# Two moves in a fused conditional-FFN kernel: the mixed 128x128 kernels get small tiles and ScalarE's DMA queue, and the inputs of the quarter products of a round's first pair are made on VectorE

## The chip, the cores and the metric

The kernel runs on one core of one Trainium2 chip. The metric is the device time of the whole program in microseconds. Before the change the median of three runs is 2623.2 us (2620.95 to 2623.56). A separate execution under the hardware profiler gives the trace.

## What is computed

The reference has two layers on x of 32 batches by 128 channels by 2048 positions, all in float32, each layer added to x. Cut to what matters:

```python
# layer 0
att   = softmax(mlp(cond))                              # 32 x 8
agg_w = einsum('bk,koi->boi', att, weight)              # a mixed 128x128 kernel for each batch
y     = einsum('boi,bih->boh', agg_w, x) + (att @ bias_k)[:, :, None]
x     = x + y @ W.T + bias + LoRA(y)                    # W is 2048 x 2048
# layer 1
z     = grouped_conv1d(x, 9 taps, 4 groups) + ctx + fside
x     = x + unpermute(ffn(permute(z)))                  # 16 heads: 128 -> 512, gelu, 512 -> 128
```

The kernel first folds the LoRA part into W, then multiplies x by W (positions by positions, 2048 by 2048), and applies the small mixed kernel of each batch afterwards, since the two products act on different axes.

## The kernel before, in words

**Rounds and steps.** The product x W is made by Strassen's scheme, two levels deep everywhere and three levels deep in part. The outer level gives seven rounds, worked in the order P1, P2, P6, P7, P5, P3, P4 (`ROUNDS`). Each round has eight steps g = 0 to 7, one for each group of four batches; `steps` lists all 56, and the main loop (L1043) goes through them. In a step of the inner level, `multiply` (L333) makes seven products of four matmuls each, 128x512, into PSUM banks, and after each product VectorE adds the bank to accumulators in SBUF (L342; in round P1 ScalarE copies the first ones, L344). After each product but the last, `between(j)` puts other work in VectorE's order.

**Pairs.** In rounds P2, P6, P7, P5 and P3 (`THIRD`) most steps come in pairs g = 0 and 1, 2 and 3, and so on (`in_pair`), which go through `multiply_third` (L426). There the inner products P2 and P4 of both steps are not made directly; they are replaced by a third Strassen level across the two steps. The even step makes its five other products (L439) and their evacuations (L435). The odd step makes its own five and between them the seven "quarter" products of the pair (L450, 128x256), which are evacuated by L458. Their order in an odd step is fixed: product P1; quarters P1 and P2; product P5; quarters P6 and P5; product P6; quarters P7 and P3; product P3; quarter P4; product P7. Quarters P1, P2 and P4 read x as it is. Quarters P6, P5, P7 and P3 read `sq`, four combinations of the two steps' x that `third_inputs` (L410, operations at L417 to L420) makes, and the weights' quarters P_q that `third_weights` (L380) makes at a round's start: eight operations of 128x256 on GpSimd (L393 to L396), and four on VectorE that `between` issues in step 0 (L1109). Quarter P6 goes into the same bank as quarter P1, so it needs that bank's evacuation.

P5 is the one round where each product is added to two accumulators (`ADDED`), so that each evacuation is two VectorE operations.

**Who makes what ahead.** At the start of a step i, GpSimd is given `x_combine` of step i+1 (L296: in P6, P7, P5 and P3 pieces at L283, then four sums at L311 to L314), then in step 0 `third_weights`, then in an even step of a pair `third_inputs` on GpSimd for all rounds but P6. In P6 `third_inputs` is on VectorE and is issued after the even step's `multiply_third` (L1137). SyncE's queue loads x (L268), partial sums (L273) and, in the middle of a round, weights of the next (L507); GpSimd combines those (L283) and at the round's end makes the weights' inner sums `inner_weights` (L245, L252 to L256).

**Slots.** All the large tiles are slots of one pool: 24 slots of 8 KB for each partition (`slot`, L82). A new tile takes a slot whose former tile has no user left in the program's order, and its first writer waits until that former tile's last users are done. The order of instructions on each engine is the program's own; nothing is rescheduled.

**The mixed kernels.** `mixed_kernel(b, ks)` (L536) makes agg_w of batch b on VectorE: one multiplication (L544) and seven multiply-adds (L546), all 128x128. `between(0)` to `between(3)` make two of the eight each. Sixteen kernels share one large slot `ags`, and when the sixteenth is finished GpSimd's queue stores them to HBM (L548) in one DMA of 1 MB. Rounds P2 to P3 make six kernels each in steps 1 to 6, b = 0 to 29; P4 makes b = 30 and 31 in its steps 0 and 1. In P4 and after it, `mix_loads` (L550) loads each kernel back as a small tile `agl` from the pool `agp` (tag "ag", two buffers).

**After the rounds** comes the convolution and the FFN (L818 and L829), interleaved; the change doesn't touch their code.

Of the kernel before, what the change touches and what calls it, by code (L numbers as in the profile page):

```python
# [8 lines left out]
FP = mybir.dt.float32  # L9
# [7 lines left out]
P = 128  # L17
B = 32
L = 2048
QW = 512  # L20
KEXP = 8
# [7 lines left out]
NCH = L // P  # L29
# [3 lines left out]
NG = B // GB  # L33
# [22 lines left out]
def adaln_ffn_kernel(  # L56
# [16 lines left out]
    nc = tc.nc  # L73
# [3 lines left out]
    agp = ctx.enter_context(tc.tile_pool(name="agp", bufs=2))  # L77
# [4 lines left out]
    def slot(name, shape=(P, L)):  # L82
        return big.tile(list(shape), FP, name=name, tag="s")
# [11 lines left out]
    def scratch(name, shape=(P, L)):  # L95
        return dram.tile(list(shape), FP, name=name, tag=name)
# [12 lines left out]
    ag_d = [scratch(f"ag_d{i}") for i in range(B // NCH)]  # L109
# [32 lines left out]
    def a_scale(h, k0, k1):  # L142
        for c in range(2):
            cols = a_sb[h][:, c, :, k0:k1]
            nc.vector.tensor_scalar(cols, cols, wsc[:, c : c + 1], None, ALU.mult)
# [139 lines left out]
    def x_loads(r, g):  # L285
        return {
            "P1": lambda: [x_load(g, 0, 0)],
            "P2": lambda: [x_load(g, 0, 1)],
            "P6": lambda: [x_load(g, 1, 0), x_load(g, 1, 1), x_load(g, 0, 0)],
            "P7": lambda: [x_load(g, 0, 0), x_load(g, 1, 0)],  # L290
            "P5": lambda: [x_load(g, 1, 0), x_load(g, 1, 1)],
            "P4": lambda: [x_load(g, 1, 1)],
            "P3": lambda: [x_load(g, 0, 1), part_load("s2", g)],
        }[r]()

    def x_combine(r, g, ts):  # L296

        a = ts[0]
        tt = nc.gpsimd.tensor_tensor
        if r == "P6":  # L300

            b, a, c = ts
            pieces(b, b, a, ALU.add)
            pieces(a, b, c, ALU.subtract)
            part_store("s2", g, a)
        if r in ("P7", "P5", "P3"):
            pieces(a, a, ts[1], ALU.add if r == "P5" else ALU.subtract)
        xa[steps.index((r, g))] = a
        s = slot(f"s_{r}{g}", (P, 4, QW))
        a11, a12, a21, a22 = a[:, 0, 0], a[:, 1, 0], a[:, 0, 1], a[:, 1, 1]  # L310
        tt(s[:, 0], a21, a22, ALU.add)  # L311
        tt(s[:, 1], s[:, 0], a11, ALU.subtract)
        tt(s[:, 2], a11, a21, ALU.subtract)
        tt(s[:, 3], a12, s[:, 1], ALU.subtract)  # L314
        return {
            "P1": a11, "P2": a12, "P3": s[:, 3], "P4": a22,
            "P5": s[:, 0], "P6": s[:, 1], "P7": s[:, 2],
        }
# [88 lines left out]
    def in_pair(r, g):  # L407
        return r in THIRD and (r, g // 2) not in SKIP
# [124 lines left out]
    ags = {}  # L533
    late, ins, pms, xgs, x1ts, va, vb, hts, open_ = {}, {}, {}, {}, {}, {}, {}, {}, {}

    def mixed_kernel(b, ks):  # L536

        if b % NCH == 0 and ks[0] == 0:
            ags[b // NCH] = slot(f"ags_{b}", (P, NCH, P))
        ag = ags[b // NCH][:, b % NCH]  # L540
        for k in ks:
            att = att_bc[:, b * KEXP + k : b * KEXP + k + 1]
            if k == 0:
                nc.vector.tensor_scalar(ag, mix[:, 0], att, None, ALU.mult)  # L544
            else:
                nc.vector.scalar_tensor_tensor(ag, mix[:, k], att, ag, ALU.mult, ALU.add)  # L546
        if b % NCH == NCH - 1 and ks[-1] == KEXP - 1:
            nc.gpsimd.dma_start(ag_d[b // NCH], ags.pop(b // NCH).rearrange("p b c -> p (b c)"))  # L548

    def mix_loads(b):  # L550
        g, tp, s = b // GB, b % GB // 2, b % 2
# [487 lines left out]
    def olds_load(i):  # L1039
        r, g = steps[i]  # L1040
        olds[i] = [old and part_load(old, g) for old, _ in ADDED[r]]

    for i, (r, g) in enumerate(steps):  # L1043
        ri = i // NG
        last_round = ri + 1 == len(ROUNDS)
        if i + 1 < len(steps):
            if i + 1 not in xs:
                xs[i + 1] = x_loads(*steps[i + 1])
            if not last_round:
                lhs[i + 1] = x_combine(*steps[i + 1], xs.pop(i + 1))  # L1050
                if r in THIRD and g == 0:
                    quarters, quarter_ops = third_weights(r, rhs)
                if in_pair(r, g) and g % 2 == 0 and r != "P6":
                    sq = third_inputs(i, nc.gpsimd)
        if i == 0:
            olds_load(0)
        if i + 1 < len(steps) and not last_round:
            olds_load(i + 1)
        ahead = i + 2 < len(steps) and ri > 0 and not last_round
        if ahead and steps[i + 2][0] != "P6":  # L1060
            xs[i + 2] = x_loads(*steps[i + 2])
        if g == NG - (1 if ri else 2) and ri < len(ROUNDS) - 1:
            nxt = inner_weights(ROUNDS[ri + 1], [nxt[kc] for kc in range(4)])

        if ri == 0:
            ks = blocks[4 + 2 * g : 6 + 2 * g]
            if ks:
                two = [wt.pop(k) for k in ks]
                w_make_two(ks, two, sa[ks[0][0]], tb[ks[0][1]])
                made.extend(ks)  # L1070
                if g == 1:
                    a_scale(1, 0, 4)
                    sa[1] = a_combine(1, nc.gpsimd.tensor_tensor)
                if g == 3:
                    part, tb[0] = b_combine(0, nc.gpsimd.tensor_tensor)
                    for _ in range(4):
                        part()
                for k, t in zip(ks, two):
                    unsummed.append((k[1], t))
                    if k[:2] == (1, 0):  # L1080
                        nxt[k[2]] = t
        elif ri + 1 < len(ROUNDS):
            for k, combine in waiting.items():
                nxt[k] = combine()
            waiting = {}
            if 2 <= g < 6:
                waiting[g - 2] = outer_weights(ROUNDS[ri + 1], g - 2)

        if last_round and g == 0:
            late_loads()  # L1090
        if last_round and g == 2:

            late["te"] = mix.rearrange("p (k r) c -> p k r c", k=2)
            nc.sync.dma_start(mix.rearrange("p k c -> p (k c)"), te_d)
        k0 = 3 * (g - NG)
        if last_round:
            stage(k0, stage_first)

        def between(j):

            g0 = g - (not last_round)
            b = (ri - 1) * (NG - 2) + g0
            if ri > 0 and 0 <= g0 < NG - 2 and b < B and j < KEXP // 2:
                mixed_kernel(b, (2 * j, 2 * j + 1))
            if ri == 0 and j == 2:
                for k in blocks[6 + 2 * g : 8 + 2 * g]:
                    wt[k] = w_load(*k)
            if r in THIRD and j < 4 and quarter_ops:
                nc.vector.tensor_tensor(*quarter_ops.pop(0), ALU.subtract)  # L1109
            if j == 3 and ahead and steps[i + 2][0] == "P6":  # L1110
                xs[i + 2] = x_loads(*steps[i + 2])
            if ri == 0 and j in (1, 3) and unsummed:
                row_sums(*unsummed.pop())
            if ri == 0 and j == 5 and unsummed_first:
                t = unsummed_first.pop(0)
                tt = nc.vector.tensor_tensor
                tt(wsum[:, 0, 0], wsum[:, 0, 0], t[:, 0, 0], ALU.add)
                tt(wsum[:, 0], wsum[:, 0], t[:, 1], ALU.add)
            if last_round:
                if j == 3 and i + 1 < len(steps):  # L1120
                    lhs[i + 1] = x_combine(*steps[i + 1], xs.pop(i + 1))
                    olds_load(i + 1)
                if j in (2, 4):
                    stage(k0 + j // 2, stage_first)
                if j % 2:
                    stage_third(k0 + j // 2)
                else:
                    stage(k0 + j // 2, stage_second)

        if in_pair(r, g):  # L1130
            multiply_third(
                r, g, lhs.pop(i), rhs, olds.pop(i), between, quarters, sq if g % 2 else None
            )
        else:
            multiply(r, g, lhs.pop(i), rhs, olds.pop(i), between)
        xa.pop(i - 1, None)
        if in_pair(r, g) and g % 2 == 0 and r == "P6":  # L1137
            sq = third_inputs(i, nc.vector)
        next(chain, None)
        if i > 5:  # L1140
            next(chain, None)
        if last_round and g >= 6:
            pair(g - 6)
        if last_round and g == 7:
            rings()
            gather_two(0)
        if g == NG - 1 and ri + 1 < len(ROUNDS):
            rhs = nxt
            nxt = {}
# [84 lines left out]
```

## Time and profile before

| | |
|---|---|
| median of the runs | 2623.2 us (2620.95 to 2623.56) |
| profiled execution, its own time | 2625.11 us |
| its span, first to last instruction | 2623.0 us |
| mean granted TensorE clock | 0.994 |
| TensorE matmul | 2590.8 us, 99% |
| VectorE | 1459.2 us, 56% |
| GpSimd | 1337.5 us, 51% |
| ScalarE | 532.9 us, 20% |
| DMA | 608.27 MB, mean 232 GB/s |

The profile has several views, and all of them are of one execution. The head of the page gives each engine's busy time and its share of the span. The waits list who waited for whom: the engine with line and tile, the releaser, the total in us, the number of times, the longest. The timeline gives the instructions of an engine in order of time, with like ones merged: start, duration, engine, line, operation, output and inputs, shape, count, and in brackets the idle time of the engine before it with what ended it. PE is TensorE, PEld its weight loads, DVE VectorE, ACT ScalarE, POOL GpSimd, SP SyncE. A float32 matmul shows as two records. The round starts, read from the first product of each round on TensorE's timeline, are P2 306, P6 494, P7 681, P5 884, P3 1077 and P4 1261 us.

### The profile page before, as it was taken

What the parts mean: (1) busy time and instruction counts of PE and PEld (TensorE: products, weight loads), DVE (VectorE), ACT (ScalarE), POOL (GpSimd) and SP (SyncE); (2) the same over time, 40 slices, a digit from 0 to 9 for tenths busy, and PEclk for the clock granted to TensorE, in tenths of its full rate; (3) what the DMA queues carried; (4) which work ended last, traced back from release to release, by engine and by line L of the source; (5) the groups of instructions that cost most, each with busy time, mean ns of one, the idle gap of its engine ahead of it and who ended that gap; (6) DMA issues with size and microseconds to landing.
All of it is one profiled execution on the core that took longest, in us unless ns stands there. A gap on an engine that the chain in (4) does not pass through costs nothing.

```text
span 2623.0 us, 21287 instructions
## 1 busy us (share of the span) xinstructions
PE 2590.8 (99%) x6876; PEld 1310.3 (50%) x6876; DVE 1459.2 (56%) x2310; ACT 532.9 (20%) x1099; POOL 1337.5 (51%) x1110
## 2 busy tenths in 40 slices
PE   9999999999998999999999999999999999999998
PEld 4444455455454555455444445555545554555543
DVE  5554155455353476454376666676666666666610
ACT  0000000000000000000011244444444444444432
POOL 7320657987975773886432334434443344444222
PEclk9999999999998999999999999999999999999999
DMA  7542458778465577566668798777777777787532
GB/s 314 213 163 109 175 210 331 270 297 335 183 246 234 193 287 297 233 246 235 214 219 260 222 311 291 233 231 221 234 234 249 251 222 225 231 252 232 165 120 88
DMA packets 183838, 608.27 MB, mean 232 GB/s; under 512 B 17200, under 2 KB 88368, under 8 KB 139440
## 3 DMA queue, kind: packets, MB, share of 16 engines
q1 hardware_dynamic: 149936, 473.74, 51.1%
q0 software_dynamic: 32992, 132.14, 14.9%
q10 hardware_dynamic: 800, 1.03, 0.1%
q8 instruction: 55, 0.90, 0.1%
q14 instruction: 55, 0.45, 0.0%
HBM read 372.45 MB, written 200.84 MB: 219 GB/s over the span
## 4 chain that ended last, share of the span: by engine, by line
PE 78%; POOL 13%; DMA 5%; issue 2%; DVE 1%; SPq 0%; POOLq 0%; ACT 0%; DVEq 0%; ACTq 0%
PE bank L818 17%; PE bank L829 16%; PE bank L349 15%; PE bank L439 13%; PE bank L674 6%; PE bank L450 5%; POOL xt L283 5%; PE bank L582 4%; PE bank L223 2%; DMA xt<-in_xT 2%; POOL wo_P L283 1%; POOL wo_P L256 1%; DMA bf_sb<-in_BfT 1%; POOL P_t L253 1%; POOL s_P L311 1%
## 5 line engine op out<-in xcount | busy, mean ns | idle before, releaser
L818 PE MATMUL bank<-t,ws 128*128 128x512 f32 x1024 | 460.4, 592 | 0.6 <-DMA ws<-in_ffw 0.6
L829 PE MATMUL bank<-gl,ws 128*128 128x512 f32 x1024 | 460.2, 592 | 0.0
L836 POOL DMA_INDIRECT out<-t,orow x128 | 151.6, 1185 | 537.5 <-DVE t L834 458.6
L821 ACT ACTIVATE gl<-bank 128x512 f32<-128x512 f32 x512 | 306.2, 598 | 446.1 <-PE bank L818 443.1
L829 PEld LDWEIGHTS bank<-gl,ws 128*128 128x128 f32 x1024 | 194.6, 190 | 233.0 <-issue 230.8
L818 PEld LDWEIGHTS bank<-t,ws 128*128 128x128 f32 x1024 | 194.5, 190 | 227.5 <-issue 222.5
L567 POOL TENSOR_TENSOR x<-x,fb 128x512 f32<-128x512 f32 x128 | 178.7, 1424 | 213.5 <-DMA x<-in_x 175.7
L573 ACT ACTIVATE bank<-w,aggb 128x512 f32<-128x512 f32 x128 | 80.8, 683 | 916.9 <-DMA w<-w_d 900.0
L834 DVE TENSOR_TENSOR t<-bank,t 128x512 f32<-128x512 f32 x128 | 88.5, 691 | 319.7 <-PE bank L829 319.7
L439 PE MATMUL bank<-P_t,s_P 128*128 128x512 f32 x544 | 241.8, 592 | 0.0
L435 DVE TENSOR_TENSOR u<-bank,u 128x512 f32<-128x512 f32 x168 | 110.7, 688 | 199.6 <-PE bank L439 186.6
L283 POOL TENSOR_TENSOR xt<-xt,xt 128x512 f32<-128x512 f32 x128 | 162.4, 1302 | 92.3 <-DMA xt<-in_xT 82.9
L311 POOL TENSOR_TENSOR s_P<-xt 128x512 f32<-128x512 f32 x56 | 72.3, 1291 | 260.6 <-DMA xt<-in_xT 169.6
L439 PE MATMUL bank<-wo_P,s_P 128*128 128x512 f32 x448 | 199.1, 592 | 0.0
L546 DVE SCALAR_TENSOR_TENSOR ags<-mix,att_bc,ags 128x128 f32<-128x128 f32 x224 | 177.1, 791 | 4.5
L439 PEld LDWEIGHTS bank<-P_t,s_P 128*128 128x128 f32 x544 | 103.4, 190 | 115.6 <-issue 111.7
L802 POOL DMA_INDIRECT t<-hx_d,row x128 | 131.4, 1027 | 50.1 <-issue 26.4
L349 PE MATMUL bank<-P_t,s_P 128*128 128x512 f32 x352 | 154.7, 592 | 0.0
L439 PEld LDWEIGHTS bank<-wo_P,s_P 128*128 128x128 f32 x448 | 85.1, 190 | 95.2 <-issue 93.5
L674 PE MATMUL bank<-va,tw_l 128*128 128x256 f32 x512 | 121.6, 380 | 0.2
L674 PEld LDWEIGHTS bank<-va,tw_l 128*128 128x128 f32 x512 | 96.8, 190 | 41.9 <-issue 31.7
L450 PE MATMUL bank<-P_q,sq 128*128 128x256 f32 x408 | 101.3, 401 | 16.4 <-DVE u L458 9.8
(189 smaller groups left out, 3563.4 us busy)
## 6 DMA issues: line engine op xcount, KB each, us to landing
xt<-in_xT SPq DMA_DIRECT2D x88, 1024.0 KB, 9.1
u<-u_d SPq DMA_DIRECT2D x40, 1024.0 KB, 8.5
wo_P<-wb_d SPq DMA_DIRECT2D x36, 1024.0 KB, 10.9
u<-c_d SPq DMA_DIRECT2D x64, 512.0 KB, 7.1
x<-in_x SPq DMA_DIRECT2D x32, 1024.0 KB, 8.5
xg<-x SPq DMA_DIRECT2D x256, 128.0 KB, 5.4
hx_d<-x1t SPq DMA_DIRECT2D x32, 1024.0 KB, 5.9
hx_d<-ht SPq DMA_DIRECT2D x32, 1024.0 KB, 7.1
```

The costliest lines, as they stand in the source:

```text
L283: nc.gpsimd.tensor_tensor(out[:, i, j], a[:, i, j], b[:, i, j], op)
L349: nc.tensor.matmul(ps, lhsT=lhs[k][:, bass.ts(kc, P)], rhs=rhs[k][kc], start=first and kc == 0, stop=last and kc == 3, skip_group_check=True,)
L439: nc.tensor.matmul(ps, lhsT=lhs[k][:, bass.ts(kc, P)], rhs=rhs[k][kc], start=first and kc == 0, stop=last and kc == 3, skip_group_check=True,)
L450: nc.tensor.matmul(out, lhsT=sq[k][:, i, bass.ts(kc, P)], rhs=quarters[i][k][kc], start=first and i == 0 and kc == 0, stop=last and i == 1 ...
L546: nc.vector.scalar_tensor_tensor(ag, mix[:, k], att, ag, ALU.mult, ALU.add)
L567: nc.gpsimd.tensor_tensor(xt[:, f], xt[:, f], late["fb"][:, f], ALU.add)
L674: nc.tensor.matmul(out, lhsT=w[:, 2 * i + r], rhs=rhs, start=first and r == 0, stop=last and r == 1, skip_group_check=True,)
L802: nc.gpsimd.indirect_dma_start(out=t.rearrange("p k t -> p (k t)"), out_offset=None, in_=hx_d[g].rearrange("l k t -> l (k t)"), in_offset= ...
L818: nc.tensor.matmul(pu, lhsT=w[:, m * P : (m + 1) * P], rhs=t[:, 0], start=True, stop=True)
L821: nc.scalar.activation(gl[m], pu, AF.Gelu)
L829: nc.tensor.matmul(pd, lhsT=w[:, (MC + m) * P : (MC + m + 1) * P], rhs=gl[m], start=(m == 0), stop=(m == MC - 1),)
L836: nc.gpsimd.indirect_dma_start(out=out, out_offset=bass.IndirectOffsetOnAxis(ap=orow[:, g, h : h + 1], axis=0), in_=t[:, 1], in_offset=None,)
```

## The change

It has two parts.

The mixed kernels no longer share large slots. Each gets a tile of 128x128 of its own from `agp`, under the tag "ag" with its two buffers, which the loads `agl` use later as well. When its eighth operation is done, the kernel is stored by a DMA of 64 KB on ScalarE's queue, 32 stores in all. The kernels also come two steps earlier in number: b = 0 and 1 in the last two steps of P1, b = 2 to 31 in steps 1 to 6 of P2 to P3, none in P4.

In the first pair of a round (g = 0) `third_inputs` is made on VectorE, after the even step's products, in P2, P7, P5 and P3 as it is in P6 already. The other pairs keep it on GpSimd, and all of P6 stays on VectorE.

```diff
     def mixed_kernel(b, ks):
 
-        if b % NCH == 0 and ks[0] == 0:
-            ags[b // NCH] = slot(f"ags_{b}", (P, NCH, P))
-        ag = ags[b // NCH][:, b % NCH]
+        if ks[0] == 0:
+            ags[b] = agp.tile([P, P], FP, name=f"ags_{b}", tag="ag")
+        ag = ags[b]
         for k in ks:
...
-        if b % NCH == NCH - 1 and ks[-1] == KEXP - 1:
-            nc.gpsimd.dma_start(ag_d[b // NCH], ags.pop(b // NCH).rearrange("p b c -> p (b c)"))
+        if ks[-1] == KEXP - 1:
+            nc.scalar.dma_start(ag_d[b // NCH][:, bass.ts(b % NCH, P)], ags.pop(b))
...
-                if in_pair(r, g) and g % 2 == 0 and r != "P6":
+                if in_pair(r, g) and g % 2 == 0 and g > 0 and r != "P6":
                     sq = third_inputs(i, nc.gpsimd)
...
         def between(j):
 
-            g0 = g - (not last_round)
-            b = (ri - 1) * (NG - 2) + g0
-            if ri > 0 and 0 <= g0 < NG - 2 and b < B and j < KEXP // 2:
+            b = (ri - 1) * (NG - 2) + g + 1 if ri > 0 else g - (NG - 2)
+            if (g in range(1, NG - 1) if ri > 0 else g >= NG - 2) and b < B and j < KEXP // 2:
                 mixed_kernel(b, (2 * j, 2 * j + 1))
...
-        if in_pair(r, g) and g % 2 == 0 and r == "P6":
+        if in_pair(r, g) and g % 2 == 0 and (g == 0 or r == "P6"):
             sq = third_inputs(i, nc.vector)
```

## The prediction

> **What bounds the kernel now.** I read the busy shares first, then the waits of TensorE, then the stretches around each of its waits on the timelines of TensorE, VectorE and GpSimd.
>
> ```profile
> PE 2590.8 (99%) x6876; PEld 1310.3 (50%) x6876; DVE 1459.2 (56%) x2310; ACT 532.9 (20%) x1099; POOL 1337.5 (51%) x1110
> ```
>
> TensorE has work in 99% of the span and no other engine is above 56%. So a change that leaves the matmuls alone can win only TensorE's idle time, and the stretches in which its clock is down. Of 32 us of idle, 9.0 are the tail after the last matmul and 3.7 the start; the rest is in a few waits. The waits of TensorE:
>
> ```profile
> PE bank L450 <- DVE u L458: 9.8, 1, 9.8
> PE bank L450 <- POOL sq L418: 6.6, 3, 3.5
> ```
>
> Both are the quarter products (L450). On TensorE's timeline, one undisturbed block of 16 records and then the four that waited:
>
> ```profile
> 333.57 3.62 PE L450 MATMUL bank<-P_q,sq 128*128 128x256 f32 x16
> ...
> 710.65 5.41 PE L450 MATMUL bank<-P_q,sq 128*128 128x256 f32 x16 [2.27 <-POOL sq L418]
> ...
> 815.23 6.66 PE L450 MATMUL bank<-P_q,sq 128*128 128x256 f32 x16 [9.78 <-DVE u L458]
> ...
> 914.78 6.39 PE L450 MATMUL bank<-P_q,sq 128*128 128x256 f32 x16 [3.51 <-POOL sq L418]
> ...
> 1105.92 3.72 PE L450 MATMUL bank<-P_q,sq 128*128 128x256 f32 x16 [0.87 <-POOL sq L418]
> ```
>
> Columns: start, duration, group, and in brackets the idle time before it with what ended it. The same 16 records take 3.62 us when nothing is wrong, so a wait costs its idle time plus what the block is longer by. The table by stretches says why they are longer; its columns are the stretch, its length with the busy time of TensorE, and the granted clock:
>
> ```profile
> 712.00:715.00 3.00, 3.00 (x8) 0.50 0.00 0
> 716.00:730.00 14.00, 14.00 (x46) 1.00 0.19 76
> 808.00:821.00 13.00, 5.77 (x14) 0.50 0.43 163
> 914.00:920.00 6.00, 5.21 (x12) 0.50 0.00 0
> 1100.00:1112.00 12.00, 11.13 (x38) 1.00 0.01 3
> ```
>
> After waits of 2.27, 9.78 and 3.51 us the clock is at half for a while; after the one of 0.87 it is not. The costs: 2.27+1.79 = **4.06** (P7, first pair), 9.78+3.04 = **12.82** (P7, third pair), 3.51+2.77 = **6.28** (P5, first pair), 0.87+0.10 = **0.97** (P3, first pair). Together 24.13 us, which is all that can be won here. Cross-check: P7 runs from 680.74 to 883.62, 202.88 us; an undisturbed pair takes 46.42 (731.38 to 777.80), four take 185.68; the excess is 17.2, and 4.06+12.82 = 16.9.
>
> Now the cause of the large one. VectorE, then GpSimd:
>
> ```profile
> 813.81 0.29 DVE L544 TENSOR_SCALAR ags<-mix,att_bc 128x128 f32<-128x128 f32 x1 [14.46 <-POOL xt L283]
> ```
> ```profile
> 793.37 0.56 POOL L548 DMA_DIRECT2D ag_d<-ags  x1 [12.54 <-DVE ags L546]
> 793.95 4.93 POOL L283 TENSOR_TENSOR xt<-xt,xt 128x512 f32<-128x512 f32 x4
> ...
> 808.85 4.92 POOL L283 TENSOR_TENSOR xt<-xt,xt 128x512 f32<-128x512 f32 x4
> ```
>
> L544 is the first step of kernel 16, which opens the second tile of sixteen and needs a large slot. In the built program that slot belongs to an xt whose last reader is the L283 group ending at 813.8. That group was late because GpSimd stood 12.54 us at the store of the first sixteen, whose last step VectorE makes only in step 4 of P7. The evacuations L458 stand behind L544 on VectorE, and TensorE waits for them.
>
> **What the Trainium skill says.** "TensorE: Matmul & The Clock Gate", Part 1: after an idle window of about 3.4 us the array goes to half clock, and needs a busy window to come back; the windows run freely. The trace agrees in kind (records of 3.4, 13.7 and 6.8 us at 0.5) though the 2.27 us wait already lost a window. "SBUF — State Buffer", Who interferes with whom: a VectorE instruction with two SBUF inputs contends with a GpSimd instruction that reads SBUF, the loser blocks; one with a PSUM input does not. The trace agrees, as shown next. "DMA: Bandwidth & Descriptors", Issuing engines are not separate DMA queues: all issue onto the same 16 engines, another issuer saves sequencer time alone; so the new queue adds no bandwidth, and I give it none.
>
> **The change, part by part.**
>
> *Small tiles.* The 256 mixing operations are the same, at the same steps of rounds P2 to P3 (kernels numbered two higher); kernels 0 and 1 move to the last two steps of P1, 30 and 31 leave P4. What goes is the wait of L544 for a large slot and both waits of GpSimd at L548 (12.54 and 17.66). The small buffer of kernel b is the one of b-2, free when that store has landed. Between the last step of b-2 and the first of b VectorE leaves at least 23.2 us (kernels 26 and 28, 1169.6 to 1192.8); the nearest row, a 32 KB store on ScalarE's queue, lands in 1.5 us, the 64 KB loads agl in a median of 5.8 and at most 13.9. Cost: nothing, covered by those 23 us. ScalarE waits in order for VectorE before each store; in P2 to P3 it is nearly idle (3.0 us busy in P2, none later), and in P1 it has four copies a step, which stand clear because the mixing is done before the store's place. In P1's last step and a half (262 to 306) VectorE is busy 4.88 of 44 us, so 2 x 8 operations of about 0.74 us = 12 us fit. Gain: **12.82**. What is late next there? sq of that pair was ready at 775.9, thirty us early, and the other waits of the stretch are evacuations of a 2.7 us cadence: nothing.
>
> *A large slot is free,* and GpSimd no longer does four sq operations in each first pair. The built program gives other slots to most tiles. I matched each tile's previous owner with its last use in the trace: most waits shrink, six DMA issues on SyncE would wait longer on the old times, the worst u3_2 by 8.3 us, with xt_301 and s2_3 queued behind it; these are next needed by GpSimd about 20 us later. P5's weight combines wait on TensorE at P7's end and start 1.4 us earlier. I take zero; both ends: one window of clock gained, or see the second rival.
>
> *sq on VectorE in the first pairs.* Taken out: 4 x 1.265 us of GpSimd in P2, P7, P5, P3, behind which its next combines stood. Added: four 128x512 operations on VectorE at the end of step 0. P6 already does this:
>
> ```profile
> 511.98 1.73 DVE L417 TENSOR_TENSOR sq<-xt 128x512 f32<-128x512 f32 x1
> 513.75 1.10 DVE L418 TENSOR_TENSOR sq<-sq,xt 128x512 f32<-128x512 f32 x1
> 514.77 1.21 DVE L419 TENSOR_TENSOR sq<-xt,xt 128x512 f32<-128x512 f32 x1
> 515.90 1.21 DVE L420 TENSOR_TENSOR sq<-xt,sq 128x512 f32<-128x512 f32 x1
> 517.04 0.68 DVE L435 TENSOR_TENSOR p<-bank,p 128x512 f32<-128x512 f32 x1
> ```
>
> 5.1 us while GpSimd makes P_q (2.8 us when it is quiet, at 605.7), and TensorE did not wait in P6. Replaying 5.1 us in the other rounds: in each, VectorE must finish the last evacuation of step 0, sq, one evacuation L435, two mixing operations and the first L458 before TensorE comes to the quarter product.
> P7: 699.4+5.1 = 704.5, +0.7+1.4+0.7 = 707.3, needed at 708.4. Wait 0.
> P3: 1096.1+5.1+0.7+1.4+0.7 = 1104.0, needed at 1105.05. Wait 0.
> P2: 324.7+5.1+0.7+2.1+0.7 = 333.3, needed at 333.57. Wait 0, margin 0.3.
> P5 has two accumulators, so evacuations are double: 903.5+5.1+1.3+1.6+1.3 = 912.8 less the 0.1 of overlap, needed at 911.27. Wait **1.35**; between 0.87 (clock held) and 2.27 (lost, +1.79) the trace has nothing, so I add half, 0.9: a remainder of 2.25.
> P_q on GpSimd slows beside sq by about 1.9 us (four of 0.72 became 1.05 to 1.18 in P6): in P7 its last needed piece moves from 706.7 to 708.6, used at 708.8. Just in time.
> Gain: 4.06 + 0.97 + (6.28 - 2.25) = **9.06**.
>
> Sum: 12.82 + 9.06 = 21.9. The profiled execution took 2625.11 (span 2623.0 and 2.1 around it), so 2603.2 for it; the median of the three runs is 1.9 lower, 2623.2, and gives **2601.3**.
>
> **Rivals.** *The first-pair stalls only change engine:* VectorE's lag replaces GpSimd's, and 4.06, 6.28 and 0.97 stay. For it: margins of 0.3 to 1.1 us. Against: P6. Time: 2623.2 - 12.8 = 2610.4. *A slot or load comes late:* SyncE held 8.3 us, a pair starved by as much with a half-clock window of 3: 2601.3+11.3 = 2612.6. Against: some 20 us of lead. *Slower:* the small stores land late. With landing T, L544 holds VectorE T-23.2 in each of some 30 steps; VectorE has 2.7 us idle before each evacuation, so TensorE loses T-25.9. It decides at 21.9/30 = 0.7, T of 26.6 us; at 28 us the loss is 63 and the time 2664. Nothing in the trace lands so late once the start is over.
>
> **How the numbers follow.** Forecast 0.78, first rival 0.12, second 0.06, slower one 0.04. The range runs from everything won (24.1) less half the spread of the runs (1.3), 2597.8, to the first rival plus 1.3, 2611.7. A measurement can tell about 0.2% (5 us) from no change: faster 0.93, same 0.03, slower 0.04, the forecast and two rivals being all more than 5 us faster, less a little for what I have not seen.
>
> **What would show it.** Right: no wait at L544 nor L548; TensorE's waits at L450 gone in P7 and P3, about 1.3 us with "DVE" as releaser in P5; the clock at 1.00 in P7. Wrong: waits at L450 ended by L458 in P2, P7 and P3; a wait of L544 ended by a DMA; a new TensorE wait on a load in P3.

## The result and the profile after

The changed kernel takes 2603.0 us (median of four runs, 2600.5 to 2604.9), the kernel before 2623.4 beside it (2621.0 to 2626.8): 20.4 us less, a ratio of 0.9921 with a 95% interval of 0.9904 to 0.9938. The prediction was 2601.3, with 2597.8 to 2611.7 as its range. The profiled execution took 2603.33, as against the 2603.2 worked out for it; its span is 2601.6.

The head of the changed kernel's page:

```profile
PE 2582.1 (99%) x6876; PEld 1304.0 (50%) x6876; DVE 1476.3 (57%) x2326; ACT 533.6 (21%) x1099; POOL 1322.5 (51%) x1092
```

TensorE executes the same 6876 records in 8.7 us less busy time, although no matmul was touched: that is half clock which is gone, 7.7 us of it in the four places of the prediction. Half clock at the start belongs to it too: 3.41 us in the profile of before, from 8.87 on, and none in this one. The rest of the gain is idle time. TensorE's waits in the changed kernel (who, for whom, us in total, times, longest):

```profile
PE bank L223 <- DVE w L226: 3.2, 3, 2.5
...
PE bank L450 <- POOL P_q L394: 1.4, 1, 1.4
...
PE bank L450 <- POOL P_q L395: 0.5, 1, 0.5
```

The waits at L450 of 2.27, 9.78, 3.51 and 0.87 us have become one of 0.5, in P5, and a new one of 1.4 in P6. On TensorE's timeline the blocks of quarter products in the first pairs of P2, P6, P7, P5 and P3 now read:

```profile
334.01 3.62 PE L450 MATMUL bank<-P_q,sq 128*128 128x256 f32 x16
...
523.37 3.29 PE L450 MATMUL bank<-P_q,sq 128*128 128x256 f32 x14 [1.44 <-POOL P_q L394]
...
710.36 3.62 PE L450 MATMUL bank<-P_q,sq 128*128 128x256 f32 x16
...
896.73 3.69 PE L450 MATMUL bank<-P_q,sq 128*128 128x256 f32 x16 [0.53 <-POOL P_q L395]
...
1084.13 3.62 PE L450 MATMUL bank<-P_q,sq 128*128 128x256 f32 x16
```

P7 and P3 are at the undisturbed 3.62 us. In the table by stretches, two rows from P7, one over P7's third pair (to be set against the 808.00 row of before) and one over P5 show the clock, the last but two of the columns, at full speed:

```profile
712.00:715.00 3.00, 3.00 (x13) 2.16 (x12) 2.67 (x4) 0.00 (x0) 2.84 (x4) 1.00 0.00 0
716.00:730.00 14.00, 14.00 (x46) 8.52 (x45) 7.97 (x10) 0.00 (x0) 13.77 (x11) 1.00 0.20 80
800.00:815.00 15.00, 15.00 (x52) 9.67 (x51) 8.62 (x11) 0.00 (x0) 14.84 (x13) 1.00 0.47 182
896.00:902.00 6.00, 5.47 (x22) 3.93 (x22) 5.96 (x9) 0.00 (x0) 6.00 (x7) 1.00 0.00 0
```

No wait of VectorE at L544 nor of GpSimd at L548 is left. So the sum came true, and every sign that was named for it but one: P5's remainder is 0.53 us, not 1.3, and the view does not name VectorE as its releaser. Whether the *parts* gave what they were credited with is another question, and the sum cannot answer it.

### The profile page after: what moved, and what is told of

It reads as the page before. It is cut to its first block, busy times and chain, and to the rows that moved or that the text cites. A ratio compares the mean times of both kernels' runs of the same rounds, so it can differ in the third digit from the quotient of the medians.

```text
span 2601.6 us, 21348 instructions
## 1 busy us (share of the span) xinstructions
PE 2582.1 (99%) x6876; PEld 1304.0 (50%) x6876; DVE 1476.3 (57%) x2326; ACT 533.6 (21%) x1099; POOL 1322.5 (51%) x1092
## 5 line engine op out<-in xcount | busy, mean ns | idle before, releaser
L435 DVE TENSOR_TENSOR u<-bank,u 128x512 f32<-128x512 f32 x168 | 110.7, 688 | 196.2 <-PE bank L439 178.1
L283 POOL TENSOR_TENSOR xt<-xt,xt 128x512 f32<-128x512 f32 x128 | 161.9, 1297 | 106.1 <-DMA xt<-in_xT 88.2
L546 DVE SCALAR_TENSOR_TENSOR ags<-mix,att_bc,ags 128x128 f32<-128x128 f32 x224 | 184.8, 825 | 4.7
L342 DVE TENSOR_TENSOR u<-bank,u 128x512 f32<-128x512 f32 x84 | 56.4, 685 | 110.0 <-PE bank L349 108.6
```

What stands on the lines that cost most here:

```text
L283: nc.gpsimd.tensor_tensor(out[:, i, j], a[:, i, j], b[:, i, j], op)
L435: nc.vector.tensor_tensor(acc[:, si, oi], ps, acc[:, si, oi], ALU.add)
```

## The experiments

Each kernel was executed 5 to 13 times, in turn with the kernel before (the changed kernel 4 times). "Against before" is the difference from the median of before in the same comparison, and the last column is the ratio with its 95% interval. "In the rounds" is read from one trace each: by how much the time from TensorE's first product of P2 to its first of P4 changes. That is 958.1 us in the kernel before, from 306.08 to 1264.22 (P4 begins there, not at 1261), and 935.8 in the changed kernel, from 306.52 to 1242.33. What nothing disturbs repeats in the rounds: P7's second pair takes 46.42 us in all fourteen traces. The start up to P2 takes 304.9 to 308.6 us and what follows the rounds 1357.1 to 1363.2, so this column tells the parts apart more sharply than the medians do.

| kernel | us | against before | in the rounds | ratio |
|---|---|---|---|---|
| changed | 2602.97 | -20.4 | -22.3 | 0.9921 (0.9904 to 0.9938) |
| small tiles alone | 2606.65 | -15.8 | -15.2 | 0.9940 (0.9926 to 0.9953) |
| quarters of x on VectorE alone | 2624.36 | +1.9 | -0.8 | 1.0006 (0.9998 to 1.0015) |
| before, store of sixteen on ScalarE's queue | 2620.32 | -2.2 | -3.9 | 0.9991 (0.9982 to 0.9999) |
| changed, small stores on GpSimd's queue | 2604.38 | -18.1 | -23.9 | 0.9931 (0.9917 to 0.9945) |
| quarters of x alone, P7's quarter weights later | 2616.85 | -6.6 | -9.9 | 0.9976 (0.9967 to 0.9986) |
| changed, a large slot held | 2609.32 | -14.2 | -15.8 | 0.9947 (0.9934 to 0.9961) |
| changed, old numbers | 2603.55 | -19.9 | -22.6 | 0.9923 (0.9909 to 0.9936) |
| changed, quarters of x made twice | 2634.16 | +10.7 | +9.4 | 1.0043 (1.0029 to 1.0057) |
| small tiles alone, P7's quarter weights later | 2604.08 | -19.6 | -19.2 | 0.9926 (0.9912 to 0.9939) |
| the same, a large slot held | 2610.27 | -12.1 | -13.8 | 0.9954 (0.9940 to 0.9967) |
| changed, P_q in another order | 2601.26 | -22.4 | -23.9 | 0.9915 (0.9901 to 0.9928) |
| changed, one small tile instead of two | 2602.12 | -21.6 | -22.5 | 0.9920 (0.9906 to 0.9933) |

### Each half by itself

The theory: 12.8 us come from the small tiles, 9.1 from the quarters of x. Rival: the halves do not add up.

**Small tiles alone.**

```diff
-                if in_pair(r, g) and g % 2 == 0 and g > 0 and r != "P6":
+                if in_pair(r, g) and g % 2 == 0 and r != "P6":
...
-        if in_pair(r, g) and g % 2 == 0 and (g == 0 or r == "P6"):
+        if in_pair(r, g) and g % 2 == 0 and r == "P6":
```

> The changed kernel with the quarters of x in the first pairs given back to GpSimd (P6 stays on VectorE): small tiles, the new queue and the new numbers alone. The prediction's sum: 12.8 us less than before, 2610.6; the waits of TensorE at L450 in the first pairs of P7, P5 and P3 (4.06, 6.28 and 0.97 with their half clock) are still there, the one of 12.8 in P7's third pair is not. The small new wait of the changed kernel in P6's first pair (1.4 us) comes, I think, from the other slots that the small tiles leave to GpSimd's sums, so it should be here too: then 2612. Rival, the two parts do not add up (GpSimd's four operations push something else late when the slots change): more than 2615, or less than 2608.

**Quarters of x on VectorE alone**, an edit of the kernel before:

```diff
-                if in_pair(r, g) and g % 2 == 0 and r != "P6":
+                if in_pair(r, g) and g % 2 == 0 and g > 0 and r != "P6":
...
-        if in_pair(r, g) and g % 2 == 0 and r == "P6":
+        if in_pair(r, g) and g % 2 == 0 and (g == 0 or r == "P6"):
```

> The kernel before with the quarters of x in the first pairs of P2, P7, P5 and P3 on VectorE, and nothing else. The sum of the prediction: 9.1 us less, 2614.3; if P5's remainder is as small as the changed kernel shows (0.5 and no loss of clock instead of 2.25), 10.8 less, 2612.6. GpSimd still stands at the store of sixteen, and VectorE at L544, so P7's third pair still loses about 12.8. No new wait in P6's first pair, if that comes from the slots. Rival, the waits of the first pairs only change engine: 2623.

The first gave 15.8 instead of 12.8, the second nothing instead of 9.1. In the second kernel the waits of the first pairs shrank just as worked out (P7 2.27 to 0.85, P5 3.51 to 1.34 with VectorE as releaser and the clock kept, P3 to none: 9.1 us with their half clock). But VectorE's timeline at the start of P7 has something new:

```profile
684.28 0.69 DVE L435 TENSOR_TENSOR u<-bank,u 128x512 f32<-128x512 f32 x1 [2.74 <-PE bank L439]
695.37 0.69 DVE L1109 TENSOR_TENSOR P_q<-P_t 128x512 f32<-128x512 f32 x1 [10.40 <-POOL xt L283]
695.98 0.68 DVE L435 TENSOR_TENSOR u<-bank,u 128x512 f32<-128x512 f32 x1
```

L1109 is the first of the four quarter weights that VectorE makes, which opens a large slot. In this program the slot's former tile is an x tile that GpSimd's L283 reads until 695.4; in the kernel before, the same operation starts at 684.98 without a wait. The edit did not touch that tile: moving `third_inputs` only changed which slots were handed to whom. The evacuations stand behind it, and TensorE waits 5.62 us and loses 3.2 more at half clock (its 16 records from 696.72 on take 10.19 us, and 7.03 undisturbed):

```profile
689.65 1.45 PE L439 MATMUL bank<-P_t,s_P 128*128 128x512 f32 x3
696.72 2.08 PE L439 MATMUL bank<-wo_P,s_P 128*128 128x512 f32 x2 [5.62 <-DVE u L435]
```

9.1 won and about 9 lost. The small tiles alone have a milder form of it in the same place: L1108 there (a line up) stands 6.71 us, and TensorE waits 2.0 us and loses 1.7 at half clock.

**The wait at the slot taken away.** In the second kernel the four quarter weights of P7 are made later, when that x tile has been read:

```diff
-            if r in THIRD and j < 4 and quarter_ops:
-                nc.vector.tensor_tensor(*quarter_ops.pop(0), ALU.subtract)
+            if r in THIRD and quarter_ops and (j >= 3 if r == "P7" else j < 4):
+                for _ in range(2 if r == "P7" else 1):
+                    nc.vector.tensor_tensor(*quarter_ops.pop(0), ALU.subtract)
```

> The kernel with the quarters of x on VectorE alone (2624.4, as slow as before), with one edit: in P7 VectorE makes the four quarter weights (L1109) two steps at a time from the fourth and fifth place of the first step, some 11 us later than now. If the 5.6 us wait of TensorE at 691 us, with some 3.4 us of half clock, comes from VectorE standing at the first of them for a large slot that GpSimd's L283 still reads until 695.4, it goes and the 9 us come back: 2615.4, which is the gain that the prediction gave to this part. Rival, moving the quarters of x gives nothing by itself and the lost time turns up elsewhere: 2624.

It took 2616.9, 6.6 us less than before (interval 3.7 to 8.7). L1110, the same operation, waits 0.22 us, and P7's first step has no wait of TensorE:

```profile
695.89 0.69 DVE L1110 TENSOR_TENSOR P_q<-P_t 128x512 f32<-128x512 f32 x1 [0.22 <-POOL xt L283]
```

The rival at 2624 falls. In the rounds the gain is 9.9 us, of which 0.8 is a shorter stretch of half clock in P7's third pair. So the quarters of x are worth about what was predicted *on the kernel before*, once a slot does not take it back.

### What made the long wait: GpSimd's queue, or the large slot?

The prediction said that kernel 16 waited 14.46 us because GpSimd had stood 12.54 us at the store of sixteen.

```diff
-            nc.gpsimd.dma_start(ag_d[b // NCH], ags.pop(b // NCH).rearrange("p b c -> p (b c)"))
+            nc.scalar.dma_start(ag_d[b // NCH], ags.pop(b // NCH).rearrange("p b c -> p (b c)"))
```

> The kernel before with one word changed: the store of sixteen goes onto ScalarE's queue; large slots, numbers and the quarters of x stay. If the long wait of VectorE at L544 comes from GpSimd standing 12.5 us at the store, as the prediction says, it goes without any small tile: 2623.4 - 12.8 = 2610.6, ScalarE waiting in its place at no cost. Rival, the large slot itself is what is late (its former tile is read late whatever the queue): 2623.

The other way round, the changed kernel with its 32 small stores on GpSimd's queue:

```diff
-            nc.scalar.dma_start(ag_d[b // NCH][:, bass.ts(b % NCH, P)], ags.pop(b))
+            nc.gpsimd.dma_start(ag_d[b // NCH][:, bass.ts(b % NCH, P)], ags.pop(b))
```

> The changed kernel with its small stores on GpSimd's queue, all else kept. GpSimd then waits, in each of the 24 steps with a kernel, for VectorE's last mixing operation in the second half of the step, and what it has to do for the step after stands behind that. If the queue is what the change is worth, some of these waits reach TensorE as the one of 12.5 us did in the kernel before: 2608 to 2640. If the small tile alone is the remedy, since nobody waits for a large slot behind the store: 2603, as the changed kernel.

The first gave 2.2 us, not 12.8. GpSimd no longer waits at the store, and still its L283 begins at almost the same time, since right behind the store it would have waited for a load of x. GpSimd, then VectorE, of the kernel before with the other queue:

```profile
791.18 5.05 POOL L283 TENSOR_TENSOR xt<-xt,xt 128x512 f32<-128x512 f32 x4 [11.11 <-DMA xt<-in_xT]
```
```profile
811.59 0.28 DVE L544 TENSOR_SCALAR ags<-mix,att_bc 128x128 f32<-128x128 f32 x1 [12.99 <-POOL xt L283]
```

The store's wait had covered the load's: 12.54 us of standing there delayed L283 by about 2 us (it began at 793.95 before, 2.8 us later, and TensorE was 0.7 us later there too). TensorE still waits at the same place:

```profile
PE bank L450 <- DVE u L458: 8.3, 1, 8.3
```

The changed kernel shows it from the other side. There, too, GpSimd waits 11.07 us for that load and ends its second group only at 810, but VectorE's L544 does not wait for it:

```profile
789.85 5.04 POOL L283 TENSOR_TENSOR xt<-xt,xt 128x512 f32<-128x512 f32 x4 [11.07 <-DMA xt<-in_xT]
...
804.95 5.04 POOL L283 TENSOR_TENSOR xt<-xt,xt 128x512 f32<-128x512 f32 x4
```

The second kernel is the counterpart. GpSimd's waits there:

```profile
POOL ag_d L548 <- DVE ags L546: 156.0, 23, 15.5
```

23 waits of 156 us in all, and the kernel takes 2604.4; its rounds are even 1.5 us shorter than the changed kernel's, since the new wait in P6 is missing. The queue is worth little: 2.2 us alone, with 0.3 to 4.7 as the interval, and nothing that can be measured in the changed kernel. What counts is that the mixed kernel no longer waits for a large slot.

### The freed slot

The prediction gave the freed large slot zero. Two kernels take it away again, without a wait for VectorE or GpSimd: ScalarE holds a slot for every sixteen kernels.

```diff
             ags[b] = agp.tile([P, P], FP, name=f"ags_{b}", tag="ag")
+            if b % NCH == 0:
+                hold[0] = slot(f"hold_{b}", (P, NCH, P))
+            nc.scalar.copy(hold[0][:, b % NCH], mix[:, 0])
```

In the changed kernel:

> The changed kernel with one large slot taken for every sixteen kernels again, which only ScalarE writes (a copy of 128x128 ahead of each kernel, added work; nothing reads it), so that VectorE and GpSimd never wait for it. This takes away the freed large slot and keeps all else. In this program VectorE's first quarter weight of P7 again follows a tile that GpSimd reads late; if the freed slot matters by that, TensorE waits 2 to 5.6 us in P7's first step, with half clock: 2607 to 2612. The prediction's zero for the freed slot: 2603, as the changed kernel.

6.3 us more than the changed kernel. With the slot held, the quarter weight of P7 follows that late x tile again. VectorE waits for it, and then TensorE for VectorE:

```profile
694.70 0.69 DVE L1113 TENSOR_TENSOR P_q<-P_t 128x512 f32<-128x512 f32 x1 [10.17 <-POOL xt L283]
```
```profile
696.04 9.06 PE L439 MATMUL bank<-wo_P,s_P 128*128 128x512 f32 x16 [5.38 <-DVE u L435]
```

So the freed slot is not worth zero. ScalarE's copies are added work, and a kernel with the copies and without the slot was not run; no wait in the traces of the two kernels is put down to these copies.

Next, small tiles alone without that stall. I expected the kernel to become *slower*, since the first-pair waits of P7 would come back:

> The small tiles alone (2606.7) with P7's four quarter weights on VectorE moved to the fourth and fifth place of the first step, which takes away its wait for the slot of a tile that GpSimd reads late (2.0 us of TensorE and 1.7 of half clock). If the small tiles alone came out 4 us better than the prediction's 2610.6 because TensorE, held there, no longer came too early for GpSimd's quarters of x in that pair, then taking the wait away brings those waits back and the kernel gets slower: 2610 to 2612. Rival, the two are independent: 2603.

That was wrong: 2604.1. With the quarters of x still on GpSimd, all that is left of TensorE's waits at L450 is:

```profile
PE bank L450 <- POOL sq L418: 2.2, 1, 2.2
...
PE bank L450 <- POOL P_q L394: 1.2, 1, 1.2
```

P7's wait of 2.27 and P3's of 0.87 are gone though nothing was done about them, and P5's is 2.2 instead of 3.5. Was that the slot? The same kernel with the slot held:

> The small tiles with the four quarter weights of P7 made later (2604.1) and with one large slot taken again for every sixteen kernels, written by ScalarE alone (added copies of 128x128, read by nobody). It asks what made GpSimd's quarters of x in the first pairs come in time there although they were still on GpSimd. If it was the freed large slot, the waits come back as in the kernel before: 3.5 us and 2.8 of half clock in P5, 0.9 in P3, and in P7 the 2.3 us less what the later quarter weights give (GpSimd's sums there took 5.8 us beside them and 4.9 without, two groups): 2607 to 2610. If it was the absence of GpSimd's waits at the store, or the later quarter weights alone, P5 keeps 2.2 us and P3 none: 2604.

2610.3, and TensorE's waits in the first pairs are back:

```profile
PE bank L450 <- POOL sq L418: 6.9, 3, 3.5
```

2.48, 3.51 and 0.88, as in the kernel before (2.27, 3.51, 0.87). How a slot does this shows on SyncE's queue ahead of P7 (start, duration of the group, then the loads and stores issued). With the slot held, the loads of x wait until 631:

```profile
619.98 1.07 SPq L507 DMA_DIRECT2D wo_P<-wb_d  x2
630.99 1.28 SPq L268 DMA_DIRECT2D xt<-in_xT  x3
```

and with the slot free the first of the three is issued at 620:

```profile
611.34 8.62 SPq L507 DMA_DIRECT2D wo_P<-wb_d  x2
620.05 11.42 SPq L268 DMA_DIRECT2D xt<-in_xT  x3
```

GpSimd's sums for the next step then begin at 636.05 instead of 638.69 in these two kernels, and so does its whole chain up to the round's boundary: `sq` starts at 705.1 instead of 707.5, with TensorE 1.5 us later (P7 begins at 681.58 instead of 680.07, most of it by the new wait in P6). Together that is more than the wait of 2.48. Counted from each round's first product, `sq` starts 3.9 us earlier in P7, 1.3 in P5 and 2.8 in P3 than with the slot held. Only the way to P7 was followed back to a load; for P5 and P3 it is taken to be of the same kind.

### Numbers, margins and the rest

**The old numbers** (kernel 0 in P2, the last two in P4):

```diff
-            b = (ri - 1) * (NG - 2) + g + 1 if ri > 0 else g - (NG - 2)
-            if (g in range(1, NG - 1) if ri > 0 else g >= NG - 2) and b < B and j < KEXP // 2:
+            g0 = g - (not last_round)
+            b = (ri - 1) * (NG - 2) + g0
+            if ri > 0 and 0 <= g0 < NG - 2 and b < B and j < KEXP // 2:
```

> The changed kernel with the old numbers: kernel 0 starts in P2 and the last two are mixed in P4's first steps, not in P1's last ones. The prediction gives the numbering nothing: 2603. Rival, the two kernels in P4, where VectorE has the attention's work too, hold something up: 2605 to 2610.

2603.6: the numbers are worth nothing that can be measured.

**The quarters of x made twice**, to see how close VectorE is to the limit; the second set is added work with the same values.

```diff
-            sq = third_inputs(i, nc.vector)
+            sq = third_inputs(i, nc.vector, 2 if g == 0 else 1)
```

with the four operations of `third_inputs` in a loop of so many times.

> The changed kernel with the four operations of the quarters made twice in the first pair of each of the five rounds (the same results, added work of about 4.2 us on VectorE in P2 and P7, 5 to 6.6 in P3, P5 and P6). It asks how near VectorE is to being what TensorE waits for there. By the changed kernel's trace VectorE is done 0.8 us early in P2 and 1.9 us in P7, so waits of about 3.4, 2.3 and in the other three 3 to 6 us should stand at L450, released by VectorE, with a few us of half clock each: 2620 to 2640. Rival, VectorE has room enough and the margins are not the limit: less than 2608.

2634.2, in the middle of that range. TensorE's waits (L451 and L459 are L450 and L458, a line down):

```profile
PE bank L451 <- DVE u L459: 11.8, 3, 5.6
PE bank L451 <- DVE p L459: 9.0, 2, 5.0
```

All five first pairs wait now, 2.8 to 5.6 us, all for VectorE. The rival that VectorE has plenty of room falls: the changed kernel is within a few microseconds of a new stall in each of the five rounds.

**One small tile** instead of two, which leaves a store only the time between two successive kernels.

```diff
-            ags[b] = agp.tile([P, P], FP, name=f"ags_{b}", tag="ag")
+            ags[b] = agp.tile([P, P], FP, name=f"ags_{b}", tag="ags", bufs=1)
```

> The changed kernel with one small tile in place of two, so that each kernel's first operation on VectorE waits for the store of the kernel just before. Between a kernel's last operation and the next one's first lie about 10 us and more, not 23. If the stores land in a few us, as the prediction held, nothing waits: 2603. If they land in over 10 us at times (its slower rival), VectorE stands at L544, released by a DMA, and TensorE behind it: above 2608.

2602.1. VectorE does wait for stores, briefly:

```profile
DVE ags L544 <- DMA ag_d<-ags: 13.3, 9, 2.3
```

Nine waits, 2.3 us at most, and none reaches TensorE. With two tiles there are none.

**P_q in another order**, for the two waits that are left: GpSimd makes what TensorE needs first, first.

```diff
                     tt(t[:, 0, kc], r12, r11, ALU.subtract)
                     tt(t[:, 1, kc], r22, t[:, 0, kc], ALU.subtract)
-                    tt(t[:, 2, kc], r22, r12, ALU.subtract)
-                    tt(t[:, 3, kc], r21, t[:, 1, kc], ALU.subtract)
+                    rest.append((t[:, 2, kc], r22, r12))
+                    rest.append((t[:, 3, kc], r21, t[:, 1, kc]))
+            for op in rest[0::2] + rest[1::2] if i == 0 else []:
+                nc.gpsimd.tensor_tensor(*op, ALU.subtract)
```

> The changed kernel with GpSimd's eight quarter-weight operations in another order: the two that TensorE's first pair needs first (L393, L394) for both halves, then the other two for both. The second L394 comes 1.4 us earlier. P6's new wait of 1.44 us at L450 should go. The 0.53 us in P5 is put down to L395 of GpSimd, but VectorE's second L458 ends 0.14 us before the products start, as it does in other versions; if VectorE is what ends it, it stays; if GpSimd, it goes. Time 2601.5, or 2601.0: the trace tells, not the clock.

P6's wait is gone. P5's stays. TensorE, GpSimd and VectorE in P5 (lines two further down than in the kernel before):

```profile
894.38 3.69 PE L452 MATMUL bank<-P_q,sq 128*128 128x256 f32 x16 [0.62 <-POOL P_q L398]
```
```profile
891.48 0.73 POOL L394 TENSOR_TENSOR P_q<-wo_P,P_q 128x256 f32<-128x256 f32 x1
892.16 1.47 POOL L398 TENSOR_TENSOR P_q<-wo_P,wo_P 128x256 f32<-128x256 f32 x2
893.59 1.41 POOL L398 TENSOR_TENSOR P_q<-wo_P,P_q 128x256 f32<-128x256 f32 x2
```
```profile
892.96 2.47 DVE L460 TENSOR_TENSOR u<-bank,u 128x512 f32<-128x512 f32 x4
```

What TensorE needs of P_q is done at 892.2, two microseconds early. The second of VectorE's four L460, which frees the bank, ends at 894.24 in the records, and the products begin 0.14 us later; in the changed kernel the same two times are 896.59 and 896.73, and with the slot held 902.18 and 902.32. So VectorE ends this wait, and the view's label names a GpSimd operation that happened to end at about the same moment. At 2601.3 us (2599.9 to 2601.5) this kernel has the lowest median of all; its 1.7 us below the changed kernel, from two comparisons with intervals that overlap, is what the trace lets one expect (P6's 1.44 us are gone), and not more than that.

## Why the prediction was right, and where its steps were not

**What can be won.** The bound of 24.13 us, TensorE's four waits with their half clock, held: no version won more. In the rounds the four places cost 24.8, since each wait also takes away the 0.17 us by which TensorE's blocks overlap in the records when nothing waits; two of these are the 0.3 us that the prediction's cross-check left open. The best version wins 23.9 of it. The bookkeeping by waits fits: for the small tiles alone, 24.13 less what is left in P7 (1.98, and 1.7 as half of the 3.41 us that the clock is down), P5 (2.20+1.7) and P6 (1.19) gives 15.4; measured 15.8, and 15.2 in the rounds.

**Small tiles, 12.82: right in size, wrong in its cause.** With the freed slot taken out of the account (small tiles, slot held, P7's quarter weights later) the gain is 12.1, and 13.8 in the rounds. Of that, 13.0 are P7's third pair; the rest is luck with the clock, since P5's wait of 3.51 us brings 3.41 us at half clock there and 6.83 before. But the step "that group was late because GpSimd stood 12.54 us at the store" fails: without that wait L544 still waited 12.99. The load of x stood behind the store's wait and would have held L283 nearly as long. The new queue by itself is worth 2.2 us, and 2.7 of the 13 in P7's third pair. L544's wait goes because a mixed kernel has a small tile of its own and needs no large slot.

**The freed slot, zero: the step that failed.** It is worth 7.5 us by the medians against before (12.1 with the slot held, 19.6 with it free), 6.2 between the two medians, and 5.5 in the rounds. SyncE issues the first of the x loads ahead of P7 eleven microseconds sooner, and GpSimd arrives earlier at the boundaries of P7, P5 and P3. I had matched each tile with its previous owner, but asked only whether a transfer would come late, not whether some would come early and cure the waits that I gave to the other half.

**Quarters of x on VectorE, 9.06: right on the kernel before, a third of it on top.** The replayed waits were good: alone it leaves 0.85 in P7, 1.34 in P5 with VectorE as releaser, none in P3, where 0, 1.35 (1.43 by its rounded terms) and 0 were worked out. That the sum is right is partly luck: P7 keeps a wait that was put at nothing, and P5 keeps the clock, for which 0.9 was taken off. But alone it is given back by another slot (+1.9 measured), and on top of the small tiles there is less to cure: with the slot free, P7 and P3 wait no more and P5 waits less. From small tiles without the stall to the full change there are 0.8 us between the gains, each against its own runs of before, with overlapping intervals. The traces tell more: in the rounds the full change is 3.1 us shorter (P5's 2.17 and 1.7 of half clock against 0.53, less 0.25 in P6). In these two executions its start is 1.0 us longer, with waits of 2.46 us there against 0.88, and what follows the rounds 1.7. The start can't be the work of this half, which begins in P2; whether what follows is more than chance is open.

So 12.8 + 0 + 9.1 = 21.9 came out as 12.1 + 7.5 + 0.8 = 20.4 by the medians and as 13.76 + 5.46 + 3.11 = 22.33 in the rounds, the first two being measured on small tiles with P7's quarter weights made later and the last as what remains. The two halves cure the same waits by different means, which is why alone, each without the slot's stall, they give 19.6 and 6.6 (19.2 and 9.9 in the rounds), and together 20.4 (22.3). That is also why the sum came out right with wrong parts: it was already close to all that TensorE's waits had to give. And the full change had luck: of the three programs that have one half, the other or both, only in the last does P7's quarter weight not wait for its slot.

**P5's remainder, 2.25.** The releaser was right, the size was not: 0.53, and no clock lost. VectorE starts the quarters of x at the same point as in the kernel with this half alone (19.77 us after the round's first product) and takes 4.94 us instead of 5.75; GpSimd begins its P_q 1.9 us earlier there.

**P6, not foreseen.** The new 1.44 us is GpSimd's last P_q coming late. It is there in the versions with the freed slot and the stores off GpSimd's queue (1.2 to 1.4), and not where the slot is held or GpSimd waits at its stores. In the changed kernel GpSimd stores a weight tile (L527) at 452.69 instead of 456.60, among three loads of x, and starts its next sums at 463.22 instead of 459.33. That the store delays the loads is my reading; it was not tried.

**The rivals.** None came about. Small stores land in time for TensorE even with half the buffers. The first rival (the stall moves to VectorE) would decide at a few microseconds more on VectorE, as the doubled quarters show.

## What to carry to other kernels

When several large tiles share one pool, any edit that adds, drops or moves a tile deals all the later slots anew; look at which tile each waiting writer now follows, and expect gains and losses far from the edit. A wait that is removed is worth only what the next wait behind it does not take back, so ask what the engine would have waited for next. And a right total proves no part of it: run each half alone, and each half with the accident of the other taken out.

## What the runs showed of the hardware

In the rounds, every stretch at half clock in the fourteen traces lasts 3.41, 6.83, 10.24 or 13.65 us: one to four times 3.41. The length of a wait alone does not tell whether the clock is lost. In P5 and P7 waits of 1.98, 2.17, 2.27 and 2.48 us lost it; at the start, a wait of 2.46 us at 38.7 us kept it in the changed kernel and one of 2.44 at 39.1 us lost it in the kernel with the old numbers. In the rounds waits up to 1.44 us never lost it. The Trainium skill's "TensorE: Matmul & The Clock Gate", Part 1, with windows that run freely, agrees in this; its window of about 3.4 us of idle is longer than the waits of 1.98 to 2.48 us that lost the clock here, and the measurement decides.

GpSimd and VectorE slow each other when both work on SBUF tiles: GpSimd's four weight subtractions (L256) took 5.83 us beside VectorE's quarter weights and 4.94 when VectorE stood still, and in the kernel that makes the quarters of x twice the second set in P2 took 6.8 us on VectorE beside GpSimd's sums of 128x512, after 4.1 for the first beside its 128x256 operations, from start to end.
